# The opening of a two-layer graph kernel: transposes and weight products set between matmul blocks, sums taken in halves, one product streamed, one sum given to GpSimd

## The chip, the cores and the metric
One core of a Trainium2 chip. The metric is the device time of one execution in microseconds (us). Before the change the median of three executions is 563.84 us (563.43 to 564.33).

## What is computed
All numbers are float32; x is 16 x 1024 x 64, adj is 1024 x 1024.

```python
# layer 0
Q = x @ Wq.T + bq;  K = x @ Wk.T + bk;  V = x @ Wv.T
score = softmax(Q @ K^T, axis=1)
score = score @ adj
x = layernorm(x + score @ V)
# layer 1: support0 = support1 = adj
x1 = adj @ x;  x2 = 2 adj @ x1 - x          # for each support
x = layernorm(x + concat(x, x1, x2, x1, x2) @ weight + bias)
```

## The kernel before
**Layout.** The nodes lie on the 128 partitions, in eight blocks of 128. The 16 batches form eight pairs p, so that a pair's 2 x 64 channels fill 128 columns. `xs` holds x, `aT` holds adj transposed; both are loaded once, in pieces, by queue SP.

**Products with adj.** A product of adj with x is done by a scheme of seven block products in place of eight (Strassen-Winograd): adj is cut in 2 x 2 blocks of 512 x 512, the operand likewise, and each of the seven products n multiplies a sum of adj blocks, `SIDE[n]`, by a sum of operand blocks, `hop.side[n]`. Products 1, 2 and 4 use plain adj blocks. On the operand's side 1, 2, 3 are plain blocks and 5, 6, 4, 7 are the sums T1, T2, T4, T3: T1 = b01 - b00, T2 = b11 - T1, T4 = b10 - T2, T3 = T2 - b00 (class `Hop`, its method `sums`, L250). Each product P1 ... P7 consists of 16 units (four output blocks i times four inner blocks k); a unit is one float32 matmul of 128 x 128 with 256 columns (`Hop.unit`, L258), which appears as two records in the trace. A product's result lies in PSUM until `Hop.evictions` (L293, L299) copies or adds it into `UY` and `u`; `FIRST` says for the first four pairs (`hop_0`) which.

**The order.** All instructions are issued in the order in which the program is written (`manual_schedule`), each engine takes its own in that order, and waits are made from the data.

**The opening**, in the order written (L566 to L612):
1. seven small matmuls on zeros (L128), during which the first loads arrive;
2. P1 into PSUM tile pu0, by `stream(1, ...)`, k outermost, as the pieces of x and adj arrive; ACT copies pu0 into `u` (L293);
3. two transposes of the weights Wq, Wk by TensorE (`pw`, L577), three small VectorE copies, and b1 centred by VectorE (L141, L142);
4. P2 into pu1, by `stream(2, ...)`;
5. on VectorE the four sums T1, T2, T4, T3 (L250, each 128 x 1024 elements);
6. eight transposes of the first pair's x by TensorE (`first_xT`, L336), four at a time, into two PSUM tiles that ACT moves into xT (L337);
7. three small matmuls for Wk^T Wq (called G), a bias and b1 (`pg`, L589 to L591), then four VectorE copies out of it (L593 to L597) into g2, gb and bias;
8. on VectorE the eviction of pu1 (L299) and the first sum of adj blocks, `sums_of_adj(3)` (L194);
9. P4 for output blocks 0 and 1 into pv0 (`product`, k innermost), then `project` of the first pair (`both`, L368: GT = G xT + gb, four matmuls of 64 x 64 with 512 columns side by side), whose four pieces are moved from PSUM by ACT (two, L382) and VectorE (two, L386); `sums_of_adj(2)` on VectorE; P4 for output blocks 2 and 3 into pv1;
10. the evictions of pv0 and pv1 by VectorE, then the first pair's first scores (L411), their maxima by VectorE (L418) and exponentials by ACT (L427);
11. P6 and P7 for output block 0 (the two `whole_run`s at the head of the main loop, L258 again). P6 needs `sums_of_adj(2)`; P7 needs T3.

PSUM tiles named `f_tile` take turns between two banks (f0, f1), so each waits until the tile two before it is read out.

**After the opening** a loop runs over the eight pairs p and eight column blocks m. In each step TensorE does scores for the next step, the weighted sum of the last one and parts of the products with adj; VectorE takes the two maxima, ACT the two exponentials. Layer 1's products and the last normalisation follow.

Of the kernel before, what the change touches and what calls it, by code (L numbers as in the profile page):

```python
# [9 lines left out]
FP = mybir.dt.float32  # L10
AF = mybir.ActivationFunctionType
ALU = mybir.AluOpType
# [14 lines left out]
def gnn_kernel(  # L27
# [13 lines left out]
    nc = tc.nc  # L41
    N, B, C = out.shape
    P = 128
# [9 lines left out]
    const = ctx.enter_context(tc.tile_pool(name="const", bufs=1))  # L53
# [10 lines left out]
    half = [slice(j * C, (j + 1) * C) for j in range(2)]  # L64
# [3 lines left out]
    def next_tag():  # L68
        f_last[0] = 1 - f_last[0]
        return f"f{f_last[0]}"  # L70

    def f_tile(name):

        return pf.tile([P, H], FP, tag=next_tag(), name=name)

    def f_other(name):

        return pf.tile([P, H], FP, tag=f"f{1 - f_last[0]}", name=name)

    def sc_tile(name):  # L80
        return psc.tile([P, N], FP, tag="sc", name=name)
# [4 lines left out]
    g2 = const.tile([P, P], FP, tag="g2", name="g2")  # L86
# [6 lines left out]
    bks = const.tile([C, 1], FP, tag="bks", name="bks")  # L93
    b1r = const.tile([1, C], FP, tag="b1r", name="b1r")
# [39 lines left out]
    ones = const.tile([1, P], FP, tag="ones", name="ones")  # L134
    nc.vector.memset(ones, 1.0)

    def centred(w):

        rows, n, _ = w.shape
        s = small.tile([P, n], FP, tag="cs", name="cs")  # L140
        nc.vector.tensor_reduce(s[0:rows], w, AX.X, ALU.add)  # L141
        nc.vector.scalar_tensor_tensor(  # L142
            w, s[0:rows, :, None].to_broadcast([rows, n, C]), -1.0 / C, w, op0=ALU.mult, op1=ALU.add
        )
# [27 lines left out]
    K4 = K8 // 2  # L172
    Q = H // 2
# [11 lines left out]
    def sums_of_adj(*which):  # L185

        for n in which:
            out, x, y, op = {
                3: (SIDE[7], SIDE[1], SIDE[7], ALU.subtract),
                2: (SIDE[6], SIDE[4], SIDE[7], ALU.subtract),  # L190
                1: (SIDE[5], SIDE[6], SIDE[1], ALU.add),
                4: (SIDE[3], SIDE[2], SIDE[6], ALU.subtract),
            }[n]
            nc.vector.tensor_tensor(out, x, y, op)  # L194

    def quarter(big_tile, h, r, c):

        t = big_tile[:, K4 * r : K4 * (r + 1), h * H + c * Q : h * H + (c + 1) * Q]
        return t.rearrange("p k (q f) -> p q k f", q=2)

    def x_quarter(h, r, c):
        q = HP * h + 2 * c
        return xs[:, q : q + 2, K4 * r : K4 * (r + 1)]

    def into(big_tile, h):

        def d(r, c, group):
            i = K4 * r + group[0]
            t = big_tile[:, i : i + len(group), h * H + c * Q : h * H + (c + 1) * Q]
            return t.rearrange("p g (q f) -> p g q f", q=2)  # L210
        return d
# [102 lines left out]
    def by_place(t):  # L314
        return t.rearrange("c (a k n) -> c a k n", k=K8, a=A4)

    def half_block(t, h):

        return t[:, ts(h, H)].rearrange("c (k b n) -> c b k n", k=K8, b=2)

    def half_place(t):
        return t.rearrange("c (b k n) -> c b k n", b=2, k=K8)
# [4 lines left out]
    def xT(p):  # L327
        if p not in XT:
            XT[p] = att.tile([P, N], FP, tag="xT", name="xT")
        return XT[p]  # L330

    def first_xT(b):

        pt = f_tile("pt")
        for k in range(4):
            nc.tensor.transpose(pt[:, ts(k, P)], xs[:, 0, 4 * b + k], ident)  # L336
        return lambda: nc.scalar.activation(  # L337
            by_place(xT(0))[:, :, 4 * b : 4 * b + 4],
            pt.rearrange("c (k a n) -> c a k n", k=4, a=A4), AF.Copy,
        )  # L340
# [15 lines left out]
            )  # L356
        return [lambda: nc.sync.dma_start(d, t)] + [lambda b=b: back(b) for b in range(A4)]

    def project(p, js, pq):


        if 0 in js:
            GT[p] = att.tile([P, N], FP, tag="GT", name="GT")

        def made():
            for b in range(2):
                for j, t in zip(js, pq):
                    nc.tensor.matmul(  # L368
                        t[half[b]], g2[half[j], half[j]], xT(p)[half[j], ts(b, H)],
                        start=True, stop=True,  # L370
                    )

        def places(vector):
            for j, t in zip(js, pq):
                for b in range(2):

                    if vector == (b == 1 if len(js) == 1 else j == 1):
                        yield half_block(GT[p][half[j]], b), half_place(t[half[b]]), gb[half[b]]

        def by_scalar():  # L380
            for g, q, bias_ in places(False):
                nc.scalar.activation(g, q, AF.Identity, bias=bias_)  # L382

        def by_vector():
            for g, q, bias_ in places(True):
                nc.vector.tensor_scalar(g, q, bias_, None, op0=ALU.add)  # L386
        return (made,), by_scalar, by_vector

    def means(p):
# [160 lines left out]
    def both(what, *args, banks=None):  # L550

        parts, *evict = what(*args, (0, 1), banks or [f_tile(f"both{j}") for j in range(2)])
        for do in parts:
            do()
        return tuple(evict)
# [5 lines left out]
    t = [quarter(XB, 0, r, c) for r, c in ((0, 1), (0, 0), (1, 0), (1, 1))]  # L561
    hop_0 = Hop(lambda r, c: x_quarter(0, r, c), into(UY, 0), t, u, FIRST)
    t = [quarter(XB, 1, r, c) for r in range(2) for c in range(2)]
    hop_1 = Hop(lambda r, c: x_quarter(1, r, c), into(UY, 1), t, u, SECOND)

    def stream(n, places):  # L566
        for k in range(K4):
            for i in range(K4):
                hop_0.unit(places[i], n, i, k, False, k == 0 and i % 2 == 0)

    pu = [sc_tile(f"pu{n}") for n in range(2)]
    stream(1, [pu[0][:, ts(i, Q)] for i in range(K4)])
    hop_0.evict(pu[0], 1, ALL, nc.scalar.copy)

    pw = f_tile("pw")
# [2 lines left out]
    wqk_o = early[0:C, 576:704].rearrange("p (s c) -> p s c", s=2)  # L578
    nc.vector.tensor_copy(wqk_o, pw[0:C, 0:P].rearrange("p (s c) -> p s c", c=C))
    wqk_d = early[0:C, 704:960].rearrange("p (s c) -> p s c", s=2)  # L580
    for j in range(2):
        nc.vector.tensor_copy(wqk_d[:, :, half[j]], wqk_o)
    centred(b1r[:, None, :])
    stream(2, [pu[1][:, ts(i, Q)] for i in range(K4)])
    hop_0.sums(1, 2, 4, 3)
    for b in range(2):
        first_xT(b)()
    pg = f_tile("pg")
    nc.tensor.matmul(pg[:, 0:C], wqk_d[:, 1], wqk_o[:, 0], start=True, stop=True)  # L589
    nc.tensor.matmul(pg[:, C : C + 1], wqk_d[:, 0], bks, start=True, stop=True)  # L590
    nc.tensor.matmul(pg[:, P : P + C], ones, b1r, start=True, stop=True)  # L591
    for j in range(2):
        nc.vector.tensor_copy(g2[half[j], half[j]], pg[half[j], 0:C])  # L593
    gb = const.tile([P, 1], FP, tag="gb", name="gb")
    nc.vector.tensor_copy(gb, pg[:, C : C + 1])
    bias = const.tile([P, C], FP, tag="bias", name="bias")
    nc.vector.tensor_copy(bias, pg[:, P : P + C])  # L597
    hop_0.evict(pu[1], 2, ALL)
    sums_of_adj(3)
    pv = [pacc.tile([P, H], FP, tag=f"acc{h}", name="pv") for h in range(2)]  # L600
    hop_0.product(pv[0], 4, (0, 1), False)
    for do in both(project, 0):
        do()
    sums_of_adj(2)
    hop_0.product(pv[1], 4, (2, 3), False)
    for h in range(2):
        hop_0.evict(pv[h], 4, (2 * h, 2 * h + 1))
    sc = [sc_tile(f"sc{j}") for j in range(2)]
# [17 lines left out]
    y = [[quarter(UY, 0, r, c) for c in range(2)] for r in range(2)]  # L626
# [45 lines left out]

    small_of = {(p, 1): (values, p - 1) for p in range(1, NP)}
    small_of.update({(p, 4): (project, p + 1) for p in range(NP - 1)})
    for p in range(NP - 2):
        for i, step in enumerate(((p + 2, 0), (p + 2, 2), (p + 2, 3), (p + 2, 5))):
# [47 lines left out]
    for p in range(NP):  # L724
        q = p - 1
        for m in range(K8):
# [27 lines left out]
            if what:  # L754
                parts, by_scalar, by_vector = what[0](*what[1:], (0,), [f_other("small0")])
# [33 lines left out]
            if what:  # L789
                parts, by_scalar, by_vector = what[0](*what[1:], (1,), [f_other("small1")])  # L790
# [38 lines left out]
    for h in range(2):  # L829
        for j in range(2):  # L830
            made = nc.tensor.matmul(
                ACC[NP - 1, h][half[j]], us[:, j], es[j][:, ts(h, H)],
                start=False, stop=True, skip_group_check=True,
            )
# [48 lines left out]
    t = [quarter(UY, 0, r, c) for r in range(2) for c in range(2)]  # L883
# [31 lines left out]
    def tiles(*tags):  # L915
        return [
            att.tile([P, N], FP, tag=tag, name=f"in_{tag}", bufs={"e": 4, "xT": 2, "GT": 2}.get(tag, 1))
            for tag in tags
        ]
# [180 lines left out]
    t = [v.rearrange("p q k f -> p (q k f)") for v in V]  # L1100
# [4 lines left out]
    t = tiles(*X[:3])  # L1105
# [111 lines left out]
    for step_, (i, cols) in enumerate((  # L1217
# [3 lines left out]
        k, p, n = wide_step(4, 1, 0, i, cols)  # L1221
# [53 lines left out]
```

## Time and profile before
| what | value |
|---|---|
| median of three | 563.84 us |
| the profiled execution | 563.61 us; its span in the trace 561.8 us, 1.81 us around it |
| TensorE (PE) busy | 552.4 us, 98% of the span |
| VectorE (DVE) busy | 437.3 us, 78% |
| ScalarE (ACT) busy | 264.4 us, 47% |
| GpSimd (POOL) busy | 113.8 us, 20% |
| granted TensorE clock | 0.999 |

Times below are us from the span's start. A line of the timeline gives an engine's start, the time from the first start to the last end of equal neighbours, the engine, source line, operation, output and input, shape, the count, and in brackets the idle time ahead of it and what ended it. An engine's rows may overlap a little at their ends, since the end of an instruction covers its last results on their way; the distance from start to start is then the measure. PEld is TensorE's load of the stationary matrix.

### The profile page before, as it was taken

What the parts mean: (1) busy time and instruction counts of PE and PEld (TensorE: products, weight loads), DVE (VectorE), ACT (ScalarE), POOL (GpSimd) and SP (SyncE); (2) the same over time, 40 slices, a digit from 0 to 9 for tenths busy, and PEclk for the clock granted to TensorE, in tenths of its full rate; (3) what the DMA queues carried; (4) which work ended last, traced back from release to release, by engine and by line L of the source; (5) the groups of instructions that cost most, each with busy time, mean ns of one, the idle gap of its engine ahead of it and who ended that gap; (6) DMA issues with size and microseconds to landing.
All of it is one profiled execution on the core that took longest, in us unless ns stands there. A gap on an engine that the chain in (4) does not pass through costs nothing.

```text
span 561.8 us, 14532 instructions
## 1 busy us (share of the span) xinstructions
PE 552.4 (98%) x6150; PEld 407.6 (73%) x6150; DVE 437.3 (78%) x734; ACT 264.4 (47%) x595; POOL 113.8 (20%) x75
## 2 busy tenths in 40 slices
PE   8999999999999999999999999999999999999995
PEld 7757677566767777777777787677678789888644
DVE  1789889888888887888888888879747465789777
ACT  1133456547655665754755576575522200032571
POOL 0000000200200200020020010002002795594685
PEclk9999999999999999999999999999999999999999
DMA  8902001022002003102201210200201400001955
GB/s 266 346 3 76 2 38 40 2 77 76 3 39 95 21 2 113 41 2 76 77 1 40 79 37 2 76 2 2 78 1 56 95 1 2 1 1 39 180 138 169
DMA packets 26371, 33.67 MB, mean 60 GB/s; under 512 B 3010, under 2 KB 19650, under 8 KB 25922
## 3 DMA queue, kind: packets, MB, share of 16 engines
q1 hardware_dynamic: 23714, 28.35, 15.3%
q0 software_dynamic: 2176, 4.19, 4.2%
q8 instruction: 48, 0.79, 0.6%
q10 hardware_dynamic: 416, 0.20, 0.1%
q14 instruction: 17, 0.14, 0.1%
HBM read 16.48 MB, written 12.06 MB: 51 GB/s over the span
## 4 chain that ended last, share of the span: by engine, by line
PE 87%; DVE 7%; ACT 2%; DMA 2%; issue 1%; SPq 0%; POOL 0%; POOLq 0%; ACTq 0%; DVEq 0%
PE p L268 20%; PE sc L411 18%; PE acc L448 16%; PE w L864 15%; PE small L529 4%; PE w L1186 3%; PE wide L864 3%; DVE nm L418 2%; PE pu L258 2%; PE small L473 2%; PE pv L258 1%; ACT e L427 1%; PE small L368 1%; PE p L258 1%; DMA aT<-in_adjT_dram 1%
## 5 line engine op out<-in xcount | busy, mean ns | idle before, releaser
L411 PE MATMUL sc<-xT,GT 64*64 64x512 f32 x1024 | 240.7, 592 | 0.2 <-ACT e L427 0.2
L448 PE MATMUL acc<-e,us 64*64 64x512 f32 x1008 | 238.9, 590 | 0.0
L427 ACT ACTIVATE e<-sc,nm 128x1024 f32<-128x1024 f32 x128 | 142.5, 1113 | 109.2 <-DVE nm L418 103.9
L418 DVE TENSOR_REDUCE nm<-sc 128x1 f32<-128x1024 f32 x128 | 155.6, 1216 | 4.0 <-PE sc L411 3.6
L495 POOL TENSOR_TENSOR rstd<-var,expo 128x16 f32<-128x16 f32 (+3 forms) x21 | 50.6, 2412 | 410.9 <-DVE var L493 410.6
L448 PEld LDWEIGHTS acc<-e,us 64*64 64x64 f32 x1008 | 70.4, 133 | 24.2 <-issue 8.1
L411 PEld LDWEIGHTS sc<-xT,GT 64*64 64x64 f32 x1024 | 69.4, 132 | 11.7 <-issue 5.2
L268 PE MATMUL p<-UY,aT 64*64 64x256 f32 x480 | 59.2, 376 | 0.0
L268 PE MATMUL p<-XB,S 64*64 64x256 f32 x480 | 57.6, 377 | 0.0
L268 PE MATMUL p<-UY,S 64*64 64x256 f32 x384 | 45.3, 377 | 0.0
L268 PE MATMUL p<-XB,aT 64*64 64x256 f32 x352 | 43.1, 377 | 0.0
L268 PEld LDWEIGHTS p<-UY,aT 64*64 64x64 f32 x480 | 34.2, 133 | 11.5 <-issue 1.6
L268 PEld LDWEIGHTS p<-XB,S 64*64 64x64 f32 x480 | 32.9, 133 | 12.7 <-issue 2.2
L529 PE MATMUL small<-w,x0T_k 64*64 64x192 f32 x384 | 39.6, 324 | 0.0
L529 PEld LDWEIGHTS small<-w,x0T_k 64*64 64x64 f32 x384 | 26.6, 133 | 12.4 <-issue 5.5
L268 PEld LDWEIGHTS p<-UY,S 64*64 64x64 f32 x384 | 27.7, 133 | 7.3 <-issue 0.7
L268 PE MATMUL p<-xs,aT 64*64 64x256 f32 x256 | 31.7, 378 | 0.0
L268 PE MATMUL p<-xs,S 64*64 64x256 f32 x256 | 31.1, 377 | 0.0
L268 PEld LDWEIGHTS p<-XB,aT 64*64 64x64 f32 x352 | 24.9, 133 | 8.3 <-issue 1.3
L877 ACT COPY own<-w 128x512 f32<-128x512 f32 x8 | 4.5, 588 | 54.6 <-PE w L864 54.6
L539 ACT ACTIVATE UY<-small 128x128 f32<-128x128 f32 x48 | 13.3, 277 | 28.6 <-PE small L529 28.6
L427 ACT ACTIVATION_READ_ACCUMULATOR e<-sc,nm 128x1 f32 x128 | 24.8, 193 | 0.0
(211 smaller groups left out, 899.2 us busy)
## 6 DMA issues: line engine op xcount, KB each, us to landing
d<-blocks SPq DMA_DIRECT2D x15, 512.0 KB, 2.6
x0T<-d SPq DMA_DIRECT2D x32, 128.0 KB, 2.9
xs<-own POOLq DMA_DIRECT2D x8, 512.0 KB, 6.9
xT<-d SPq DMA_DIRECT2D x28, 128.0 KB, 2.8
out_dram<-xs SPq DMA_DIRECT2D x14, 256.0 KB, 2.2
xs<-in_x_dram SPq DMA_DIRECT2D x3, 1024.0 KB, 7.9
aT<-in_adjT_dram SPq DMA_DIRECT2D x8, 256.0 KB, 5.1
aT<-in_adjT_dram SPq DMA_DIRECT2D x4, 512.0 KB, 7.5
```

The costliest lines, as they stand in the source:

```text
L258: nc.tensor.matmul(po[t * w : (t + 1) * w], SIDE[n][:, k, j : j + w], self.side[n][:, :, k, :], start=start, stop=True, skip_group_check=True,
L268: nc.tensor.matmul(po[half[c]], SIDE[n][half[t], k, i * P + c * C : i * P + (c + 1) * C], self.side[n][half[t], :, k, :], start=t == 0 and ...
L411: nc.tensor.matmul(sc[half[c], ts(h, H)], GT[p][half[j], c * H + m * C : c * H + (m + 1) * C], xT(p)[half[j], ts(h, H)], start=True, stop= ...
L418: nc.vector.tensor_reduce(nm, sc, AX.X, ALU.max, negate=True)
L427: nc.scalar.activation(e, sc, AF.Exp, bias=nm, accum_out=sm[:, j : j + 1])
L448: nc.tensor.matmul(ACC[p, h][half[j]], us[half[t], j], es[j][half[t], ts(h, H)], start=m == 0 and t == 0, stop=m == K8 - 1, skip_group_che ...
L473: nc.tensor.matmul(o[half[t], ts(k, C)], OT[p][half[j], n : n + C], wv2[half[j], half[j]], start=True, stop=True,)
L495: nc.gpsimd.tensor_tensor(rstd, var, expo[:, 0:n], ALU.pow)
L529: nc.tensor.matmul(t[half[c], 0:3, k], X0T[p][half[j], n : n + C], w3[half[j]], start=True, stop=True,)
L539: nc.scalar.activation(part(UY, j), t[:, 0], AF.Copy)
L864: nc.tensor.matmul(po[:, ts(g, b.shape[1] * P)], a[:, k, ts(g, P)], b[:, :, k, :], start=start and g == 0 and k == 0, stop=True, skip_grou ...
L1186: nc.tensor.matmul(po, SIDE[n][:, k, ts(i, P)], B_F[n][:, k, cols], start=k == 0, stop=k == K4 - 1)
```

## The change
- `stream` can run a function after a given k. Four of the first pair's transposes go into P1 after its third k, the other four into P2 after its first k. `pg` and its four VectorE copies (together `weights`) go into P2 after its third k.
- The sums T1, T2, T4 are made in two halves (k = 0, 1, then k = 2, 3), each sum 128 x 512, all three of the first half before those of the second. They are written behind `stream(2)`, and so, on VectorE, behind the four copies of `weights`. T3 is one sum on GpSimd.
- Both `sums_of_adj(3, 2)` stand ahead of P4. P4 is done by `stream`, k outermost for all four output blocks, with `project` of the first pair after its second k. All four pieces of GT are moved by ACT.
- From the evictions of pv on, each engine's instructions stand in the order they had.

```diff
-    def project(p, js, pq):
+    def project(p, js, pq, all_scalar=False):
...
-                    if vector == (b == 1 if len(js) == 1 else j == 1):
+                    if vector == (not all_scalar and (b == 1 if len(js) == 1 else j == 1)):
...
+        if all_scalar:
+            return (made, by_scalar), None, None
...
-    def stream(n, places):
+    def stream(n, places, then={}):
         for k in range(K4):
             for i in range(K4):
                 hop_0.unit(places[i], n, i, k, False, k == 0 and i % 2 == 0)
+            if k in then:
+                then[k]()
+    def sums_by_half(k):
+        b, side = hop_0.b, hop_0.side
+        for o, x, y in (
+            (side[5], b(0, 1), b(0, 0)), (side[6], b(1, 1), side[5]), (side[4], b(1, 0), side[6]),
+        ):
+            o, x, y = (t[:, :, 2 * k : 2 * k + 2] for t in (o, x, y))
+            nc.vector.tensor_tensor(o, x, y, ALU.subtract)
...
+    def weights():
+        pg = f_tile("pg")
...
+        for j in range(2):
+            nc.vector.tensor_copy(g2[half[j], half[j]], pg[half[j], 0:C])
+        nc.vector.tensor_copy(gb, pg[:, C : C + 1])
+        nc.vector.tensor_copy(bias, pg[:, P : P + C])
...
-    stream(1, [pu[0][:, ts(i, Q)] for i in range(K4)])
+    stream(1, [pu[0][:, ts(i, Q)] for i in range(K4)], {2: lambda: first_xT(0)()})
...
-    stream(2, [pu[1][:, ts(i, Q)] for i in range(K4)])
-    hop_0.sums(1, 2, 4, 3)
-    for b in range(2):
-        first_xT(b)()
-    pg = f_tile("pg")
...
+    stream(2, [pu[1][:, ts(i, Q)] for i in range(K4)], {0: lambda: first_xT(1)(), 2: weights})
+    for k in range(2):
+        sums_by_half(k)
+    nc.gpsimd.tensor_tensor(hop_0.side[7], hop_0.side[6], hop_0.b(0, 0), ALU.subtract)
     hop_0.evict(pu[1], 2, ALL)
-    sums_of_adj(3)
+    sums_of_adj(3, 2)
     pv = [pacc.tile([P, H], FP, tag=f"acc{h}", name="pv") for h in range(2)]
-    hop_0.product(pv[0], 4, (0, 1), False)
-    for do in both(project, 0):
-        do()
-    sums_of_adj(2)
-    hop_0.product(pv[1], 4, (2, 3), False)
+    def first_g():
+        pq = [f_tile(f"both{j}") for j in range(2)]
+        for do in project(0, (0, 1), pq, all_scalar=True)[0]:
+            do()
+    stream(4, [pv[i // 2][:, ts(i % 2, Q)] for i in range(K4)], {1: first_g})
```

More of the change, by code (lines that the diff above doesn't have):

```diff
@@ L569, in stream @@
                 hop_0.unit(places[i], n, i, k, False, k == 0 and i % 2 == 0)
+            if k in then:
[7 more added lines that the diff above has]
+            nc.vector.tensor_tensor(o, x, y, ALU.subtract)
+    gb = const.tile([P, 1], FP, tag="gb", name="gb")
+    bias = const.tile([P, C], FP, tag="bias", name="bias")
+    def weights():
+        pg = f_tile("pg")
+        nc.tensor.matmul(pg[:, 0:C], wqk_d[:, 1], wqk_o[:, 0], start=True, stop=True)
+        nc.tensor.matmul(pg[:, C : C + 1], wqk_d[:, 0], bks, start=True, stop=True)
+        nc.tensor.matmul(pg[:, P : P + C], ones, b1r, start=True, stop=True)
+        for j in range(2):
+            nc.vector.tensor_copy(g2[half[j], half[j]], pg[half[j], 0:C])
+        nc.vector.tensor_copy(gb, pg[:, C : C + 1])
+        nc.vector.tensor_copy(bias, pg[:, P : P + C])
     pu = [sc_tile(f"pu{n}") for n in range(2)]
-    stream(1, [pu[0][:, ts(i, Q)] for i in range(K4)])
+    stream(1, [pu[0][:, ts(i, Q)] for i in range(K4)], {2: lambda: first_xT(0)()})
     hop_0.evict(pu[0], 1, ALL, nc.scalar.copy)
@@ L583, in gnn_kernel @@
     centred(b1r[:, None, :])
-    stream(2, [pu[1][:, ts(i, Q)] for i in range(K4)])
-    hop_0.sums(1, 2, 4, 3)
-    for b in range(2):
-        first_xT(b)()
-    pg = f_tile("pg")
[L589 to L597, printed above, removed]
+    stream(2, [pu[1][:, ts(i, Q)] for i in range(K4)], {0: lambda: first_xT(1)(), 2: weights})
+    for k in range(2):
+        sums_by_half(k)
+    nc.gpsimd.tensor_tensor(hop_0.side[7], hop_0.side[6], hop_0.b(0, 0), ALU.subtract)
     hop_0.evict(pu[1], 2, ALL)
-    sums_of_adj(3)
+    sums_of_adj(3, 2)
     pv = [pacc.tile([P, H], FP, tag=f"acc{h}", name="pv") for h in range(2)]
-    hop_0.product(pv[0], 4, (0, 1), False)
-    for do in both(project, 0):
-        do()
-    sums_of_adj(2)
-    hop_0.product(pv[1], 4, (2, 3), False)
+    def first_g():
[3 more added lines that the diff above has]
+    stream(4, [pv[i // 2][:, ts(i % 2, Q)] for i in range(K4)], {1: first_g})
     for h in range(2):
```

## The prediction, made before the changed kernel was run
> **What bounds the kernel now.** I read the page first (busy shares, the chain that ended last), then the waits of TensorE, then the timeline of the first 36 us, engine by engine, because the change touches nothing later.
>
> ```profile
> PE 552.4 (98%) x6150; PEld 407.6 (73%) x6150; DVE 437.3 (78%) x734; ACT 264.4 (47%) x595; POOL 113.8 (20%) x75
> PE 87%; DVE 7%; ACT 2%; DMA 2%; issue 1%; SPq 0%; POOL 0%; POOLq 0%; ACTq 0%; DVEq 0%
> ```
>
> TensorE is busy for all but 9.4 us, and 87% of the chain is its own work. A busy TensorE need not be at its peak, but the opening can be judged by pitches, start to start.
>
> ```profile
> 1.05 3.25 PE L128 MATMUL idle<-g 128*128 128x128 f32 x14 [1.05 <-DVE g L87]
> 6.86 5.42 PE L258 MATMUL pu<-xs,aT 128*128 128x256 f32 x24 [0.81 <-DMA aT<-in_adjT_dram]
> 12.54 7.17 PE L258 MATMUL pu<-xs,aT 128*128 128x256 f32 x32
> 19.55 1.04 PE L336 MATMUL pt<-ident,xs 128*128 128x128 f32 x8
> 20.83 0.43 PE L589 MATMUL pg<-early 64*128 64x64 f32 x2 [0.25 <-ACT xT L337]
> 21.73 3.72 PE L258 MATMUL pv<-XB,aT 128*128 128x256 f32 x16
> 25.38 1.09 PE L368 MATMUL both<-xT,g 64*64 64x512 f32 x8
> 26.40 3.72 PE L258 MATMUL pv<-XB,aT 128*128 128x256 f32 x16
> 30.05 1.95 PE L411 MATMUL sc<-xT,GT 64*64 64x512 f32 x16
> ```
>
> P2's 16 units take 19.55 - 12.54 = 7.01 us, 0.438 each. Each half of P4 takes 3.65 us with the switch to the next form, `both` 1.02. From 6.86 on there is one wait only, the 0.25 ahead of `pg`, which needs the PSUM bank that ACT is emptying. So 0.25 us is all that rearranging TensorE's opening can win directly; the transposes and `pg` are moved, not removed.
>
> VectorE in the same stretch:
>
> ```profile
> 16.34 1.23 DVE L250 TENSOR_TENSOR XB<-xs 128x1024 f32<-128x1024 f32 x1 [2.65 <-DMA xs<-in_x_dram]
> 17.60 2.48 DVE L250 TENSOR_TENSOR XB<-xs,XB 128x1024 f32<-128x1024 f32 x2
> 20.00 1.22 DVE L250 TENSOR_TENSOR XB<-XB,xs 128x1024 f32<-128x1024 f32 x1
> 21.84 0.47 DVE L593 COPY g<-pg 64x64 f32<-64x64 f32 x2 [0.62 <-PE pg L591]
> 22.53 1.21 DVE L299 TENSOR_TENSOR UY<-pu,u 128x1024 f32<-128x1024 f32 x1
> 32.03 1.23 DVE L418 TENSOR_REDUCE nm<-sc 128x1 f32<-128x1024 f32 x1 [0.29 <-PE sc L411]
> ```
>
> The sums start at 16.34, when x has come, and T4 (third) is done at 20.08, 1.65 us before P4 wants it at 21.73. The four copies come later, 21.84 to 22.53. VectorE still waits for TensorE at 32.03: it carries no debt into the loop.
>
> **The change, part by part.** The order of the built program's instructions shows that on VectorE the four copies of `pg` now stand ahead of all halves of the sums. This is the step that decides: P4 waits for sums that are queued behind a wait for `pg`.
>
> *When `pg` runs.* Transposes, P1, weight transposes and 12 of P2's 16 units now precede it. Before, `pg` could have started at 20.83 - 0.25 = 20.58 without its wait; four units less give 20.58 - 4 x 0.438 = 18.83. Its old wait is gone: the bank's earlier tile is read out long before. The early transposes need ident and blocks of x that P1 itself has used; the first needs its block 3 one k early, which came in the same load as block 2.
>
> *When TensorE reaches P4.* `pg` costs 21.73 - 20.83 = 0.90, the last four units 1.75: 18.83 + 0.90 + 1.75 = 21.48, the old 21.73 less 0.25.
>
> *When T4's first half is ready.* The first copy began 21.84 - 20.83 = 1.01 after `pg`: now 19.84. The copies hold VectorE for 22.53 - 21.84 = 0.69: 20.53. A half-size sum with two SBUF inputs takes 0.68 (later rows of 128 x 512, such as the L948 sums on VectorE, 0.676 to 0.692); one that reads the sum before it starts 17.60 - 16.34 - 1.23 = 0.03 after its end. Three in a chain: 3 x 0.68 + 2 x 0.03 = 2.10, so 22.63. TensorE followed VectorE by 0.04 at the start (the zeros end at 1.01, the first matmul starts at 1.05): P4 starts at **22.67**. It waits 22.67 - 21.48 = 1.19, a new wait, and starts 22.67 - 21.73 = **0.94 later** than before. Queued behind this wait on TensorE are all of P4, `both` and the first scores; nobody can fill it.
>
> *P4 and `project`.* Eight units, `both`, eight units: 3.65 + 1.02 + 3.65 as before, with `both` at 26.32 and the scores at 30.99. The second half of P4 needs T4's second half, done 2.1 us after the first at about 24.7, while TensorE comes at 27.34: covered. GT's two pieces leave VectorE (1.53 us) for ACT. ACT began 26.52 - 25.38 = 1.14 after `both`; four pieces at 0.70 (1.39 for two, the last 0.69) end at 26.32 + 1.14 + 3 x 0.70 + 0.69 = 30.25, and the scores want the last at 30.99: hidden by P4's second half with 0.74 to spare, cost 0.
>
> *The other VectorE work.* After the halves (24.7): eviction of pu1 (1.21) and the two adj sums (2.28 each) end at about 30.4. P6 needs the last; it ran at 31.93, now 32.86: 2.4 us of cover. Both halves of pv now end together at 31.0, their evictions (1.29) end at 32.3, and the scores end at 32.94: maxima not late.
>
> *T3 on GpSimd.* One instruction of 128 x 1024, waited for by P7, which started at 33.70, now 34.6. GpSimd starts it after T2's second half, about 24.0. The trace has this operation at half the size:
>
> ```profile
> 462.15 1.27 POOL L948 TENSOR_TENSOR in_o<-aT,in_t 128x512 f32<-128x512 f32 x1
> 495.84 2.13 POOL L948 TENSOR_TENSOR in_o<-S,in_t 128x512 f32<-128x512 f32 x1
> 496.77 1.75 DVE L948 TENSOR_TENSOR in_oT<-UY 128x512 f32<-128x512 f32 x1
> 498.05 1.60 POOL L948 TENSOR_TENSOR in_o<-in_o,S 128x512 f32<-128x512 f32 x1
> 500.82 0.68 DVE L879 TENSOR_TENSOR own<-w,own 128x512 f32<-128x512 f32 x1
> ```
>
> Alone it takes 2.5 (2 x 1.27), at worst 4.5 (2 x 2.27, the slowest such row): done by 26.5 to 28.5, hidden behind P4. But the two engines hold each other up: VectorE's sum at 496.77 took 1.75 in place of 0.68 beside GpSimd's, while the one at 500.82, which reads PSUM, stayed at 0.68. VectorE's delay by T3 is therefore between nothing and T3's own 4.5 less the 1.2 of the pu1 eviction (which reads PSUM), 3.3. I take 1.1, the excess of the row at 496.77, as the nearest: it fits into the 2.4 of cover, cost 0.
>
> The Trainium skill has two rules on these places. GPSIMD Engine Reference, 1. Specifications, says that GpSimd's way to SBUF is shared with VectorE, with contention where a VectorE instruction has two SBUF inputs; it speaks against the change, and taken to the full every moment of T3 beside the adj sums would be lost, which my upper bound already covers. TensorE: Matmul & The Clock Gate, Part 1, says that the clock halves only after an idle window of about 3.4 us; by it the new wait costs nothing in clock, where this trace alone can vouch only for 0.81 us.
>
> *The sum.* -0.25 for the old wait, +1.19 for the new: **+0.94 us**, say 0.9. After the scores every engine's order is unchanged, TensorE carries the chain, and no load is still under way that could fix a time, so the shift should reach the end whole. Against the profiled execution: 563.61 + 0.9 = 564.5 (span 561.8 to 562.7, with the same 1.81 around it). That execution lies 0.23 below the median of 563.84; a median should come out at 563.84 + 0.9 = **564.7**.
>
> **The rivals.**
>
> *A. No wait at P4, or the shift is absorbed* (-0.25 to +0.5; 563.6 to 564.3). It would need the halves done by 21.48, so the copies out of the way, or slack in the loop. For it: x is there at 16.34, VectorE idles until 19.84. Against it: VectorE takes its instructions in order. Chance 0.12.
>
> *B. Slower: GpSimd's T3 delays VectorE beyond its cover.* Place: the adj sums ahead of P6, and behind them the evictions of pv and the first maxima. It decides from a delay of 2.4 us on; at the bound of 3.3, P6 and the maxima lose a further 0.9. Total +1.2 to +1.8: 565.0 to 565.6. For it: 0.68 against 1.75. Against: half of T3 runs beside an eviction that reads PSUM. Chance 0.15.
>
> *C. The new wait slows TensorE's clock.* The 0.81 wait at 6.05 did no harm: the 12 units after it took 0.448 each, and the granted clock is 9 in every slice. But 1.19 is longer. At the start TensorE ran at half pace: 14 records of 128 columns at a pitch of 0.22, which later serves for 256; that lasted 3 us. Such a spell again would cost 1.5: 564.7 + 1.5 = 566.2. Chance 0.06.
>
> *D. Faster: the loop repays the work taken off VectorE*, 1.22 (T3) and 1.53 (GT), where the chain runs through VectorE (the chain's 7%). At most -2.7 + 0.9 = -1.8: 562.0. Against it: VectorE waits at 32.03, so nothing of it was owed. Chance 0.07.
>
> **The numbers.** The forecast, +0.5 to +1.25, holds 0.60 and the other cases 0.40. A measurement of this kernel tells about 0.2% from no change, 1.13 us. Faster: D, 0.07. Slower: B and C, 0.21, and the upper edge of the forecast, 0.08: 0.29. The same: 0.64. The range 563.5 to 565.6 takes in the forecast, A and B; C and D, 0.13, stay out.
>
> **What will show it.** The first P4 matmul sits at about 22.7 behind a wait of about 1.2 on VectorE's L583; no wait ahead of `pg`, which starts near 18.8; the first half sum on VectorE near 20.5, each 0.68; GT's four pieces by ACT end ahead of the scores, which start near 31.0 (before: 30.05). GpSimd's L616 takes 2.5 to 4.5. From there on every row should stand about 0.9 later than before. I am wrong if P4 starts before 22, if the wait is there but the loop's rows come back to their old times, or if TensorE's pitch changes after the wait.

## The result and the profile after
The changed kernel takes 564.97 us (median of 18), the kernel before 563.71 on the same chip: ratio 1.0021, 95% interval 1.0015 to 1.0028, so 1.26 us slower. A second sample on another chip gave 564.59 against 563.75, ratio 1.0015 (1.0006 to 1.0024), 0.84 us. The profiled execution, one of the first sample, took 565.36 us, with a span of 563.6.

TensorE's timeline of the changed kernel, in the form shown in the prediction:

```profile
7.67 3.69 PE L258 MATMUL pu<-xs,aT 128*128 128x256 f32 x16 [0.85 <-DMA aT<-in_adjT_dram]
...
19.50 0.43 PE L591 MATMUL pg<-early 64*128 64x64 f32 x2
...
20.39 1.99 PE L258 MATMUL pu<-xs,aT 128*128 128x256 f32 x8
23.37 3.72 PE L258 MATMUL pv<-XB,aT 128*128 128x256 f32 x16 [0.98 <-DVE XB L583]
27.02 1.09 PE L368 MATMUL both<-xT,g 64*64 64x512 f32 x8
28.04 3.72 PE L258 MATMUL pv<-XB,aT 128*128 128x256 f32 x16
31.69 1.95 PE L413 MATMUL sc<-xT,GT 64*64 64x512 f32 x16
```

The wait ahead of `pg` is gone, and a new one stands ahead of P4, for VectorE's half sums (L583). The row says 0.98, counted from the end of the last results of P2. From start to start, which is what the path feels, it is a little longer. Where P4 follows without a wait, it starts 1.83 after P2's last four units (22.08 - 20.25 in run 1 below), so TensorE could have begun P4 at 20.39 + 1.83 = 22.22 and began at 23.37: 1.15. Its own rows behind the wait have their old distances: P4 to scores is 31.69 - 23.37 = 8.32, before 30.05 - 21.73 = 8.32.

VectorE in the changed kernel, and GpSimd's T3:

```profile
20.50 0.46 DVE L595 COPY g<-pg 64x64 f32<-64x64 f32 x2 [5.67 <-PE pg L593]
20.97 0.16 DVE L596 COPY gb<-pg 128x1 f32<-128x1 f32 x1
21.05 0.21 DVE L597 COPY bias<-pg 128x64 f32<-128x64 f32 x1
21.18 0.68 DVE L583 TENSOR_TENSOR XB<-xs 128x512 f32<-128x512 f32 x1
21.89 1.42 DVE L583 TENSOR_TENSOR XB<-xs,XB 128x512 f32<-128x512 f32 x2
...
25.28 1.22 DVE L299 TENSOR_TENSOR UY<-pu,u 128x1024 f32<-128x1024 f32 x1
26.42 3.32 DVE L194 TENSOR_TENSOR aT<-aT 128x2048 f32<-128x2048 f32 x1
29.77 2.29 DVE L194 TENSOR_TENSOR S<-aT 128x2048 f32<-128x2048 f32 x1
```

```profile
24.73 2.86 POOL L616 TENSOR_TENSOR XB<-XB,xs 128x1024 f32<-128x1024 f32 x1 [23.42 <-DVE XB L583]
```

The bracket of the first copy matters: VectorE idles 5.67 us until `pg` is done, with all half sums queued behind. The chain that ended last goes through exactly these rows; here it is in order of time (start, length, engine and line):

```profile
20.11 0.37 PE pg L593 x2
20.48 0.02 issue
20.50 0.04 DVE g L595
20.54 0.19 issue
20.73 0.23 DVE g L595
20.96 0.01 issue
20.97 0.16 DVE gb L596
21.13 0.13 DVE bias L597
21.26 0.61 DVE XB L583
21.87 0.02 issue
21.89 0.70 DVE XB L583
22.60 0.02 issue
22.62 0.70 DVE XB L583
23.32 0.04 issue
23.37 3.72 PE pv L258 x16
```

In the profile of before the chain stayed on TensorE at this place. The profile's excess of 1.8 us in span adds up: 0.81 because the second block of adj landed later (TensorE goes on at 7.67, before at 6.86), 0.83 between there and P4 (15.70 against 14.87), nothing from P4 to the scores, 0.16 from the scores to the end (531.9 against 531.75). Only the 0.83 is work of the change. The orders do not differ up to that second block, and the same place lay at 6.95 in the second sample's profile and at 7.88 in run 3, which edits the kernel before; from the scores to the end the second sample's profile takes 563.0 - 31.31 = 531.69, no longer than before.

### The profile page after: what moved, and what is told of

It reads as the page before. It is cut to its first block, busy times and chain, and to the rows that moved or that the text cites. A ratio compares the mean times of both kernels' runs of the same rounds, so it can differ in the third digit from the quotient of the medians.

```text
span 563.6 us, 14537 instructions
## 1 busy us (share of the span) xinstructions
PE 553.5 (98%) x6150; PEld 409.0 (73%) x6150; DVE 436.7 (77%) x734; ACT 265.8 (47%) x597; POOL 116.7 (21%) x76
## 4 chain that ended last, share of the span: by engine, by line
PE 86%; DVE 7%; DMA 2%; ACT 2%; issue 1%; SPq 0%; POOL 0%; POOLq 0%; ACTq 0%; DVEq 0%
PE p L268 20%; PE sc L413 18%; PE acc L450 16%; PE w L886 15%; PE small L531 4%; PE w L1208 3%; PE wide L886 3%; DVE nm L420 2%; PE small L475 2%; PE pu L258 2%; PE pv L258 1%; ACT e L429 1%; PE small L368 1%; PE p L258 1%; DMA aT<-in_adjT_dram 1%
```

## The experiments
The theory: P4 waits for half sums that stand behind `pg`'s copies in VectorE's order (the expectations call it the queue theory). Rivals: T3 on GpSimd holds VectorE up; GT by ACT is late; the first loads are later because of the change; transposes between blocks cost something of their own. In runs 3 and 4 the kernel before is edited, in the others the changed kernel (run 5 is the changed kernel as it is). The text quoted under each edit is what was expected before the run. Ratios are to the kernel before on the same chip, with their 95% intervals in brackets.

**1. The sums ahead of the copies.**
```diff
+    def halves():
+        for k in range(2):
+            sums_by_half(k)
...
-    stream(2, [pu[1][:, ts(i, Q)] for i in range(K4)], {0: lambda: first_xT(1)(), 2: weights})
-    for k in range(2):
-        sums_by_half(k)
+    stream(2, [pu[1][:, ts(i, Q)] for i in range(K4)], {0: lambda: first_xT(1)(), 1: halves, 2: weights})
```


> The changed kernel with one move: the six half sums are written behind P2's second k, so that on VectorE they stand ahead of the four copies of pg. Queue theory (P4 waits because the half sums stand behind the copies, which wait for pg): the halves start when x has landed, about 16.3 us, six of 0.68 end near 20.6, the copies follow, P4's wait of 0.98 us is gone, and the kernel loses the whole excess: 0.25 us under the kernel before, ratio to before 0.9996 (1.26 us under the changed kernel). Contention theory (T3 on GpSimd costs the time): T3 stays, so the ratio stays near 1.002. Theory of the first loads (the changed kernel's second block of adj landed 0.81 us later in its profile, 7.53 against 6.72, and this belongs to the change): the order up to P1's third k is unchanged from the changed kernel, so about 0.8 us of loss would stay, ratio 1.001 or more.

Measured: 563.30 us, ratio 0.9994 (0.9985 to 1.0003). The half sums start at 18.72, not at 16.3 as expected, since the load that they wait for came later in this execution, but the first three are done at 20.87, in time. The wait at P4 is gone from the timeline:

```profile
20.25 1.99 PE L258 MATMUL pu<-xs,aT 128*128 128x256 f32 x8
22.08 3.62 PE L258 MATMUL pv<-XB,aT 128*128 128x256 f32 x16
```

T3 is still on GpSimd, GT still with ACT, and the transposes lie where the change put them. One move in VectorE's order takes the whole loss away: the theory holds, and the theory of the first loads falls.

**2. T3 back to VectorE.**
```diff
-    nc.gpsimd.tensor_tensor(hop_0.side[7], hop_0.side[6], hop_0.b(0, 0), ALU.subtract)
+    nc.vector.tensor_tensor(hop_0.side[7], hop_0.side[6], hop_0.b(0, 0), ALU.subtract)
```


> The changed kernel with T3 given back to VectorE, behind the six halves and ahead of the eviction of pu1. Queue theory: VectorE gets 1.22 us more work there but its adj sum of 3.32 us falls back to 2.28; the cover ahead of P6 was about 1.5 us in the changed profile (last adj sum ends at 32.06, P6 starts at 33.57), so nothing moves: ratio to before 1.002, like the changed kernel. Contention theory: the loss was made by GpSimd and goes with it: ratio 1.000 or less.

Measured: 564.45 us, 1.0015 (1.0006 to 1.0024); P4's wait is again 0.98. The first adj sum falls from 3.32 to 2.28 us, so GpSimd did hold VectorE up by 1.04 us, but nothing waited for it. The 1.000 or less of the contention theory lies outside the interval. Against the first sample of the changed kernel (1.0021) a weaker effect of T3 was left open; run 5 bears on it.

**3. The kernel before, its sums behind the copies.**
```diff
-    hop_0.sums(1, 2, 4, 3)
     for b in range(2):
         first_xT(b)()
...
     nc.vector.tensor_copy(bias, pg[:, P : P + C])
+    hop_0.sums(1, 2, 4, 3)
```


> The kernel before with one move: the four full sums T1, T2, T4, T3 are written behind the four copies of pg; nothing else is changed, no halves, no GpSimd. Queue theory, at more than the double: the copies end at 22.53 us, the third sum 3 x 1.23 + 2 x 0.03 = 3.75 later at 26.3, so P4 starts at 26.3 in place of 21.73: 4.6 us slower, ratio 1.008. Contention and GT by ACT: neither is in it, so ratio 1.000. If the loop could take back a late start, less than 4.6.

Measured: 570.67 us, 1.0123 (1.0108 to 1.0139), 6.9 us slower; the expected 1.008 lies outside. The wait is as worked out, but the units behind it are slow:

```profile
27.22 5.10 PE L258 MATMUL pv<-XB,aT 128*128 128x256 f32 x16 [4.50 <-DVE XB L250]
32.25 1.09 PE L368 MATMUL both<-xT,g 64*64 64x512 f32 x8
```

P4 starts 27.22 - 21.75 = 5.47 after `pg`, before 0.90: +4.57, the 4.6 expected. But its first half takes 32.25 - 27.22 = 5.03 in place of 3.65, +1.38: the granted clock, by stretches of 2 us from 26 on, is 0.66, 0.50, 0.99. Together 5.95. The profile's further 0.9 lies in its first loads (`pg` starts at 21.75, before at 20.83); why the median too is 0.9 above 5.95 stays open. A part may be the clock: of the four executions the two longest (570.90 and 570.99) have the lowest mean granted clock, 0.992 and 0.990 against 0.995.

**4. The kernel before, only its transposes moved into P1 and P2.**
`stream` gets its `then` as in the change.
```diff
...
-    stream(1, [pu[0][:, ts(i, Q)] for i in range(K4)])
+    stream(1, [pu[0][:, ts(i, Q)] for i in range(K4)], {2: lambda: first_xT(0)()})
...
-    stream(2, [pu[1][:, ts(i, Q)] for i in range(K4)])
+    stream(2, [pu[1][:, ts(i, Q)] for i in range(K4)], {0: lambda: first_xT(1)()})
     hop_0.sums(1, 2, 4, 3)
-    for b in range(2):
-        first_xT(b)()
```


> The kernel before with the eight transposes of the first pair inside P1 and P2, as in the change, and nothing else: pg and its copies stay behind P2, the sums stay ahead of the copies. Queue theory: only the wait of 0.25 us ahead of pg goes, ratio 0.9996 (between 0.999 and 1.000). If transposes between matmul blocks cost something of their own (a switch of form, a later load), the ratio is above 1.0000; the theory of the first loads would give 1.001.

Measured: 563.37 us, 0.9995 (0.9986 to 1.0003): the old wait goes, and transposes between blocks cost next to nothing: P2 with four of them takes 20.88 - 13.34 = 7.54, where P2 alone took 7.01 and four transposes take 0.43 (11.63 - 11.20 in the changed kernel), 0.1 more. That part of the change does what it can do, and it is small.

**5. The changed kernel again.** No edit.

> The changed kernel again, on the chip of the next three, for a second sample of its time and of its first loads. Queue theory: P4's wait is 0.98 us as in its first profile, and 0.98 - 0.25 = 0.73 us is all that the change costs: ratio to the kernel before 1.0013, and what was measured above it (1.26 us) came from the landing of the first loads or from the chip. Contention theory in its weaker form (T3 on GpSimd costs about half a microsecond, since with T3 on VectorE the ratio was 1.0015 against 1.0021): ratio 1.0021 again.

Measured: 564.59 us, 1.0015 (1.0006 to 1.0024), the same ratio as with T3 on VectorE. P4's wait is 0.98 again. So T3 on GpSimd is not shown to cost the kernel anything, though an effect of some tenths of a microsecond would not show in these intervals, and the 1.26 us of the first sample is not shown to differ from 0.84: the intervals overlap.

**6. Full sums in place of halves, behind the copies.**
```diff
-    for k in range(2):
-        sums_by_half(k)
+    hop_0.sums(1, 2, 4)
```


> The changed kernel with T1, T2, T4 as three full sums in place of six halves, still behind the copies of pg. Queue theory: P4 waits for 3 x 1.23 + 2 x 0.03 = 3.75 us of sums in place of 2.10, so its wait grows by 1.65 to 2.6 us and the kernel by as much: 2.4 us over the kernel before, ratio 1.0042. Clock: 2.6 us lies between the wait of 0.98 that left the pitch alone and the one of 4.50 after which the granted clock was 0.50 for some 2.5 us; if it halves the clock as well, another 1.4 us, ratio 1.0067. Contention theory: unchanged against the changed kernel, 1.002.

Measured: 567.94 us, 1.0073 (1.006 to 1.0087): the sum with the clock, 1.0067, is inside, the one without, 1.0042, is not. TensorE's row, and then the stretches around it; their columns are stretch and its length, busy time (and count) of PE, PEld, DVE, ACT and POOL, granted clock, DMA share, GB/s:

```profile
24.48 5.12 PE L258 MATMUL pv<-XB,aT 128*128 128x256 f32 x16 [2.58 <-DVE XB L250]
```

```profile
23.00:24.00 1.00, 0.00 (x0) 0.00 (x0) 0.97 (x2) 0.00 (x0) 0.75 (x1) 0.97 0.95 349
24.00:25.00 1.00, 0.52 (x1) 0.50 (x2) 1.00 (x2) 0.00 (x0) 1.00 (x1) 0.50 0.99 340
25.00:26.00 1.00, 1.00 (x4) 0.75 (x3) 1.00 (x2) 0.00 (x0) 1.00 (x1) 0.50 1.05 442
26.00:27.00 1.00, 1.00 (x4) 0.82 (x3) 1.00 (x1) 0.00 (x0) 0.64 (x1) 0.50 0.99 418
27.00:28.00 1.00, 1.00 (x5) 0.83 (x5) 1.00 (x1) 0.00 (x0) 0.00 (x0) 0.82 0.55 229
28.00:29.00 1.00, 1.00 (x6) 0.88 (x5) 0.96 (x2) 0.00 (x0) 0.00 (x0) 1.00 0.16 66
```

P4's first half takes 29.53 - 24.48 = 5.05, 1.40 over 3.65. In stretches of 0.02 us the granted clock falls to 0.50 at 23.94, 2.04 after the row of P2 ends (19.91 + 1.99 = 21.90) and while TensorE still waits, and is back at 27.35: 3.41 us, of which 2.87 fall on P4, and half of 2.87 is 1.4. In run 3 the same view shows the fall at 26.64, 3.92 after the end of `pg`, and the return at 30.05: again 3.41 us, 2.83 of them on P4.

**7. GT's second two pieces back to VectorE.**
```diff
-        for do in project(0, (0, 1), pq, all_scalar=True)[0]:
+        parts, by_scalar, by_vector = project(0, (0, 1), pq)
+        for do in (*parts, by_scalar, by_vector):
             do()
```


> The changed kernel with GT's second two pieces given back to VectorE; on VectorE they then stand behind both adj sums. The pieces by ACT were hidden in the changed kernel (they end at 30.97, the scores start at 31.69). Queue theory: VectorE comes to its two pieces only when the second adj sum ends, 31.98, and is through at 33.5; the second scores would then start about 1.3 us late, ratio about 1.004. If ACT's four pieces were the cause of the loss, the ratio falls below that of the changed kernel.

Measured: 566.27 us, 1.0046 (1.0033 to 1.0058). The pieces on VectorE run from 31.54 to 33.07, and the scores take 3.85 us from start to the next form in place of 1.88. So with both adj sums ahead of P4, GT by ACT saves about 1.7 us (566.27 - 564.59): a cover that is needed, not a loss.

**8. Sums ahead of the copies, and T3 on VectorE.** The edits of runs 1 and 2 together.

> The changed kernel with the half sums ahead of the copies of pg, and T3 on VectorE. Queue theory: no wait at P4, T3 hidden: 0.25 us under the kernel before, ratio 0.9996, as with T3 on GpSimd (0.9994). Contention theory in its weaker form: faster than that one by up to half a microsecond, ratio 0.9987.

Measured: 563.29 us, 0.9992 (0.9983 to 1.0001), as with T3 on GpSimd.

**9. Four half sums ahead of P4 in place of three.** T1, T2, T4 stand for each sum's output and two inputs.
```diff
-    for k in range(2):
-        sums_by_half(k)
...
+    for (o, x, y), k in ((T1, 0), (T1, 1), (T2, 0), (T4, 0), (T2, 1), (T4, 1)):
+        o, x, y = (t[:, :, 2 * k : 2 * k + 2] for t in (o, x, y))
+        nc.vector.tensor_tensor(o, x, y, ALU.subtract)
```


> The changed kernel with the six half sums in another order behind the copies: T1 first half, T1 second half, T2 first half, T4 first half, then the other two; P4 waits for four sums in place of three. Queue theory: the wait, 1.23 us from where TensorE could have started P4 in the changed kernel, grows by one sum of about 0.65 to 1.9 us; without more, 0.83 + 0.65 = 1.5 us over the kernel before, ratio 1.0026. Clock: 1.23 us of wait left the clock at 1.00, 2.83 halved it for about 3 us and cost 1.4. If 1.9 us is enough too, the wait is followed by a granted clock of 0.50 and the first half of P4 takes 5.0 in place of 3.65 us, ratio 1.0051. In between, if it depends on more than the wait's length, some executions would show it and some not: a wider spread of the times.

Measured: 565.26 us, 1.0029 (1.002 to 1.0039), 1.6 us over before, as the queue alone gives. The wait is half a microsecond longer (by the 1.83 of run 1 it is 23.32 - 19.87 - 1.83 = 1.62 from start to start, not the 1.9 expected), and the pitch behind it is unharmed (26.97 - 23.32 = 3.65; the granted clock is 1.00):

```profile
23.32 3.72 PE L258 MATMUL pv<-XB,aT 128*128 128x256 f32 x16 [1.46 <-DVE XB L620]
26.97 1.09 PE L368 MATMUL both<-xT,g 64*64 64x512 f32 x8
```

**10. Run 8 again.**

> The version with the half sums ahead of the copies and T3 on VectorE once more, on another chip, to see whether it beats the kernel before: its ratio was 0.9992 (0.9983 to 1.0001). Queue theory: it only saves the old wait ahead of pg, 0.25 to 0.4 us, ratio 0.9993 to 0.9996. If the interval again reaches 1, no version here is shown to be faster.

Measured: 563.35 us, 0.9993 (0.9985 to 1.0002). Four runs without the wait at P4 (1, 4, 8, 10) lie 0.3 to 0.5 us under the kernel before, each with an interval that reaches 1. They beat the changed kernel; that one of them beats the kernel before was not shown by itself.

## Why the prediction was right, point by point
- **The deciding step held.** VectorE's order puts the sums behind the wait for `pg`; P4 waits for them, and nothing fills the wait. Runs 1, 3, 6 and 9 move the time with the number of sums in the queue, from none to the full ones.
- **Sizes.** From `pg` to P4 I had 22.67 - 18.83 = 3.84; measured 23.37 - 19.50 = 3.87. The wait in it was 1.15 from start to start, 1.19 in the sum. Forecast for the whole shift +0.94; measured, apart from the loads, +0.83. The term that was off is the start of `pg`: I took the end of the transposes, 20.58, for the moment at which the next instruction could start, but that end includes results on their way. Four transposes take 0.43 from start to start and their row 0.60, so the eight, with a row of 1.04, take about 0.87: `pg` could have started at 20.42, and its old wait was 0.41 in this count, not 0.25. Counted from the end of the first load wait, `pg` came after 19.50 - 7.67 = 11.83, not 18.83 - 6.86 = 11.97.
- **How large.** The forecast, +0.94, was 0.17%, within bounds of +0.5 and +1.25. The first sample, 1.26, lies at the upper bound and just over the 1.13 us that I took for the least change to be told from none; the second, 0.84, lies below that. Both intervals hold 0.17%. By its number alone the first sample would fit rival B (+1.2 to +1.8) too; the rows decide against B, as said below. My absolute times hang on the first loads of one profile: P4 stood at 23.37 and 22.99 in the two profiles of the changed kernel, not at 22.67.
- **What was hidden stayed hidden.** GT's four pieces ended at 28.16 + 2.81 = 30.97, 0.72 ahead of the scores (0.74 expected). The last adj sum ended at 32.06, P6 started at 33.57; the cover was 1.5, not 2.4, since T3 had cost the first adj sum 1.04 (1.1 taken).
- **Rival A** (no wait) did not happen; run 1 shows its condition, the sums out of the copies' way. **Rival B** was right in mechanism and stayed below its point of decision: T3 took 2.86 and delayed VectorE by 1.04, nearly all of the 27.59 - 26.42 = 1.17 for which it ran beside the first adj sum; P6 did not wait. GPSIMD Engine Reference, 1. Specifications, of the Trainium skill names contention with VectorE's instructions of two SBUF inputs: this trace agrees, 3.32 against 2.28, while the pu1 eviction, with one input in PSUM, kept its 1.22 beside T3. The row at 500.82, which I read as such a case, shows nothing of it: GpSimd's sum beside it ended at 499.62 + 1.26 = 500.88. The sum at 495.00, by the same line L879, is one: it took 0.69 beside GpSimd's of 494.49 to 495.76. **Rival D** did not happen: from the scores on, everything stood later by the same amount (531.9 and, in the second sample, 531.69 to the end, against 531.75).
- **Rival C** had the right price (1.5; measured 1.4), and its condition was not met: 0.98 and 1.46 us of wait (by the rows) left the clock alone, and 2.58 halved it. TensorE: Matmul & The Clock Gate, Part 1, of the Trainium skill speaks of an idle window of about 3.4 us; in run 6 the clock fell after 2.04 us of idleness, so the measurement decides.

## What to carry to other kernels
When work is moved forward on one engine, look at what the move puts ahead of what on the engines that read its result: four copies of 0.69 us in all, set ahead of sums whose x had long come, took the sums out of their cover; they began at 21.18. In the profiles of before and of runs 1, 4, 8 and 10, where the first sum waits for a load, a later load on SP (the second of L121) starts within 0.01 us of that sum; in the changed kernel's profile it starts at 16.41, 4.8 us ahead of the sums, so x was probably there by then. On a path that is one engine's dense work, rearranging it can win no more than its waits, here 0.25 us by the row and 0.41 from start to start; read the waits first, and check that the new order makes none. Halving the sums was good repair of a bad order (it saved 3.35 us against full ones). Whether it is still of use with the sums ahead of the copies was not tested: from 18.72 in run 1 three full sums (3.75) would end at 22.47, 0.4 after P4's start at 22.08, and from 17.02 in run 10 at 20.77, in time.

## What the runs showed of the hardware that was not expected
- In waits of 2.58 and 4.50 us TensorE's granted clock fell to 0.50, for 3.41 us each time, at a price of 1.4 us; after 0.98 and 1.46 us it stayed at 1.00. The fall came 2.04 us after TensorE's last work in the one and 3.92 us after it in the other, so these profiles show no fixed length of idleness that sets it off. The price was the same because in both the fall came 0.5 to 0.6 us ahead of the next matmul. A wait's price is therefore not proportional to its length.
- The first loads vary from execution to execution with the same order of instructions up to there: where TensorE still waited for adj's second block, it went on at 6.60, 6.71, 6.86, 6.95, 7.12, 7.67 and 7.88 us. The loads that the sums wait for were there at 16.34 in the profile of before, at 16.58, 17.02, 18.11 and 18.72 in runs 4, 10, 8 and 1. Where no wait for a load is listed, the start is uneven too: in runs 6, 9 and 10 P1's first twelve units take 6.46 to 6.50 us, where the last twelve took 5.38 in the profile of before; their first records last up to 0.63 to 0.65 in place of 0.38, though the granted clock is given as 1.00 there. In a comparison of single profiles such differences have to be taken out before a change is priced.
- A GpSimd sum of 128 x 1024 with two inputs took 2.86 us and delayed VectorE's sum of two SBUF inputs beside it by 1.04 us, nearly as long as the two ran together (1.17). In run 6, where VectorE's two-input sums went on for 1.17 beside its start (here for 0.64), it took 3.38.
